# A two-layer graph network: messages laid out in steps of 32 columns, edge networks in two row halves, inputs a chunk ahead

## The chip, the cores and the metric

One core of a Trainium2 chip runs the whole program. The metric is device time in microseconds (us) of one execution. Engines are named as the profile names them: PE (TensorE) with its weight loads PEld, DVE (VectorE), ACT (ScalarE), POOL (GpSimd) and SP (SyncE, which issues most plain DMAs).

## The reference, cut to what matters

Two message-passing layers run over the same graph of N = 6250 nodes and E = 200,000 edges, sorted by destination. A node row x has 160 numbers: 64 scalars and 32 vectors of three components. Each layer mixes the rows linearly, gathers the mixed row of every edge's source, weights it by a small network of the edge's own inputs, multiplies by the edge's four attributes, sums per destination, mixes again, adds to x and normalizes. The message part of layer 0:

```python
weight = silu(edge_length_embedded @ W_fc1) @ W_fc2      # 10 -> 100 -> 192
w0, w1, w2, w3 = split(weight, [64, 128, 160])
gs, gv = x1s[edge_src], x1v[edge_src]
mid0a = w0 * gs * e_s
mid0b = w3 * (einsum('euc,ec->eu', gv, e_v) / SQRT3)
mid1a = w1[:, :, None] * gs[:, :, None] * e_v[:, None, :]
mid1b = w2[:, :, None] * gv * e_s[:, :, None]
agg = segment_sum(concatenate([...]), edge_dst) / sqrt(16)
```

Layer 1 has the network 64 -> 64 -> 224 and one more message, w5 * cross(gv, e_v). All arithmetic is fp32.

## The kernel before, in words

**Tiles and units.** The edges are cut into 1563 tiles of 128. The loop of `windows(i, ...)`, one call per layer, goes over units of four tiles, that is two pairs. Tiles are put in 284 groups of 12 down to 3 neighbouring tiles; the destinations of a group fit into a window of 32 nodes. Groups are short at the end, because destinations grow sparse in edges there and a window then holds fewer tiles: the last 220 tiles or so come in groups of three, so a unit there ends one or two groups.

**What a unit does.** The loop body issues, in this order, for unit u:
- `gather` (L665) of unit u+4: per tile one indirect DMA issued by POOL, which fetches 128 source rows of 160 numbers. The tile `g` has 8 buffers, each of a pair, so POOL can be four units ahead of the products.
- `weights` of unit u+2: per tile one matmul of hidden values by the second weight matrix into the PSUM tile `pw` (3 buffers of a pair).
- `hidden` of unit u+3: the first matrix on the inputs `e`, into the PSUM tile `pa` (1 buffer), then Silu on ACT (L624 in layer 0, L636 in layer 1). In layer 0 this is one matmul of 512 columns; in layer 1 the inputs of the first and the second pair lie in rows 0 to 63 and 64 to 127, and it is one of 256 columns.
- `places` (L699) and `products` (L681, L686) of unit u+2 on DVE. `places` makes per tile a 128 x 4 x 32 selector: one-hot of the edge's place in the window times one attribute. `products` makes the messages `mid`, not yet times an attribute: one instruction of 256 columns, and two (layer 0) or three (layer 1) of 192.
- `aggregate` of unit u on PE: selector of one attribute (32 columns, as weights) times a stretch of `mid`, summed in the PSUM tile `pg`; attribute c goes to partitions 32c to 32c+31, that is to column group c of the array. Layer 0 has six matmuls per tile (of 160, 96, 64, 64, 32 and 32 columns), layer 1 seven (160, 64, 96, 128, 96, 64, 32). When a group ends, ACT copies the sums to `r` (L728, L730).
- `turn` of the groups that ended in the unit before: PE transposes `r` into the PSUM tile `pt` (1 buffer; in layer 1 also four small matmuls), and DVE adds it to the standing sums `sm` and `sr` (L749, L751) at a place read from a register (L746).
- a step of node work. When all edges of a block of 128 nodes are in, `second_nodes` (layer 0) or `last_nodes` (layer 1) runs `summed`, `turn`, `mix` for it, one step a unit, through the PSUM tile `pn`. Its rows go to the table from which the next layer gathers.

**What sets the order.** PE keeps the order of the code (`keep_in_program_order`); the other engines get theirs from the scheduler of the framework, and each runs its queue in order. Two uses of one PSUM bank are kept apart by waits. Layer 1 can gather only when all rows of layer 0 are in the table, so the two layers do not overlap on POOL. The e inputs are DMAs of SP (L598, L607), issued in `hidden` when a chunk is first used: in layer 0 a chunk is one unit in three buffers, in layer 1 two units in two buffers. src indices and attributes come 48 tiles at a time (L578, L579).

**The prologue** makes layer 0's table (`turn_nodes`, `send_nodes`; PSUM tiles `pw`, `pa`, `pg`, `pn`, `pt`), checks the windows, and builds the weights `rm0`, `rr0` (copies L377 to L384) and `rm1`, `rr1` (16 small SP DMAs at L406, scaled at L411). L134 and L139 are the helpers through which all matmuls and transposes go, so the profile shows these two lines for PE, and tiles must be told apart by their names. The function `general` is for other graphs and does not run here.

Of the kernel before, what the change touches and what calls it, by code (L numbers as in the profile page):

```python
# [9 lines left out]
F32 = mybir.dt.float32  # L10
I32 = mybir.dt.int32
AF = mybir.ActivationFunctionType
OP = mybir.AluOpType
# [73 lines left out]
def kernel(ctx: ExitStack, tc: tile.TileContext, a, out):  # L87
# [17 lines left out]

    nc = tc.nc
# [5 lines left out]
    dram = ctx.enter_context(tc.tile_pool(name="dram", bufs=1, space=bass.MemoryType.DRAM))  # L112

# [62 lines left out]

    iota = const.tile([P, W], F32, name="iota")
# [22 lines left out]
    nc.gpsimd.dma_start(fc1[0][:10], a["W_fc1"])  # L200
# [35 lines left out]
    def turn_nodes(bs, x):  # L236
# [7 lines left out]
        z = psum.tile([P, 512], F32, name="pa", bufs=1)  # L244
# [11 lines left out]
    def send_nodes(bs, xt, zt):  # L256
# [3 lines left out]
        for j in range(len(bs)):  # L260
            tag, k = (("pg", 2), ("pn", 1), ("pg", 2), ("pt", 1))[j]
            p = psum.tile([P, 512], F32, name=tag, bufs=k)
            q = p[:n, :2 * D].rearrange("p (w d) -> p w d", w=2)
            matmul(q[:, :, 0:P], xt[:, j * P:j * P + n], l1, start=True, stop=True)
            qs.append(q)
# [50 lines left out]
    def checked():  # L316
        p = psum.tile([P, 512], F32, name="pa", bufs=1)
# [51 lines left out]
    for j in range(2):  # L369
# [3 lines left out]
        for k in range(2):  # L373
# [5 lines left out]
    nc.vector.tensor_copy(rm0[0:64, 1:4, :, S:],  # L379
                          q[0:64, None, :, S:].to_broadcast([64, 3, 2, V]))  # L380
    nc.vector.tensor_copy(rm0[64:96, 1:4, :, 0:S],
                          q[64:96, None, :, 0:S].to_broadcast([32, 3, 2, S]))
# [10 lines left out]
    for at, n, f in ((0, 160, 0.125), (160, 32, r3 / 8), (192, 32, r2 / 8)):  # L393
# [4 lines left out]
    pieces = [(rm1[0:64, 0, ss], l2s[0:64]), (rm1[64:96, 0, vx], l2v[64:96]),  # L398
              (rm1[96:128, 0, vy], l2v[64:96]), (rr1[0:32, vz], l2v[64:96])]
    pieces += [(rr1[32 * c:32 * c + 32, ss], l2s[64:96]) for c in (1, 2, 3)]  # L400
    pieces += [(rm1[0:64, 1 + c, v], l2v[0:64]) for c, v in enumerate((vx, vy, vz))]

    for c, v0, v1 in ((1, vz, vy), (2, vz, vx), (3, vy, vx)):
        pieces += [(rm1[64:96, c, v0], l2v[96:128]), (rm1[96:128, c, v1], l2v[96:128])]
# [3 lines left out]
    for o, f in ((rm1[:, :, 0:96], fs), (rm1[:, :, 96:], fv), (rr1[:, 0:96], fs),  # L408
                 (rr1[:, 96:], fv), (rm1[64:96, 1, vz], -1.0), (rm1[96:128, 2, vx], -1.0),
                 (rm1[64:96, 3, vy], -1.0)):  # L410
        nc.vector.tensor_scalar(o, o, f, None, op0=OP.mult)  # L411
# [95 lines left out]
    def last_nodes(b, work, clear):  # L507
# [10 lines left out]
        def summed():  # L518
# [5 lines left out]
            for c in (1, 2, 3):  # L524
                matmul(q[:, 96:192], sm[:, c, rows], rm1[:, c, 96:192], start=False, stop=(c == 3))
# [20 lines left out]
    def windows(i, loads, work):  # L546
        nw = (192, 224)[i]

        at_c, at_d, at_f, at_a, at_b, wid = ((0, 64, None, 160, 224, 320),
                                             (0, 160, 64, 256, 320, 416))[i]  # L550

        if i == 0:
            sums = [(0, at_a, 0, 1, 160, 0), (1, 0, 0, 1, 96, 0), (2, 0, 0, 1, 64, 0),
                    (3, 0, 0, 1, 64, 0), (2, at_d + V, 0, 1, V, 64), (3, at_d + 2 * V, 0, 1, V, 64)]
        else:
            sums = [(0, at_a, 0, 1, 160, 0), (1, 0, 0, 1, 64, 0), (2, 0, 0, 1, 96, 0),
                    (3, 0, 0, 1, 128, 0), (1, at_f + V, 0, 1, 96, 64),
                    (2, at_f + 2 * V, 2 * V, 2, V, 96), (3, at_d + 2 * V, 0, 1, V, 128)]
        made = {}
        ec = (EC // 2, EC)[i]  # L560

        inputs_of = None
        if i == 0:

            inputs_of = [loads.tile([P, EC * P // 2], F32, name=f"e{k}", bufs=1) for k in range(3)]
            for e in inputs_of:
                nc.vector.memset(e, 0.0)
# [24 lines left out]
        def inputs(c):  # L592

            e0 = c * ec * P
            n = min(ec * P, E - e0)
            if i == 0:
                e = inputs_of[c % 3]
                nc.sync.dma_start(e[:10, :n], a["e10"][:, e0:e0 + n])  # L598
            else:

                e = loads.tile([P, EC * P // 2], F32, name="e", bufs=2)
                for u in range(0, n, 4 * P):
                    for h in range(2):
                        r = u + h * 2 * P
                        m = min(2 * P, n - r)
                        if m > 0:
                            nc.sync.dma_start(e[h * 64:h * 64 + 64, u // 2:u // 2 + m],  # L607
                                              a["e64"][:, e0 + r:e0 + r + m])
            made["e", c] = e

        def hidden(u):

            t0 = 4 * u
            c = t0 // ec
            if ("e", c) not in made:
                inputs(c)
            e = made["e", c]
            n = min(4 * P, E - t0 * P)
            p = psum.tile([P, 512], F32, name="pa", bufs=1)
            h = work.tile([P, 512], F32, name="h", bufs=2)  # L620
            at = (t0 % ec) * P
            if i == 0:
                matmul(p[:100, :n], fc1[0], e[:, at:at + n], start=True, stop=True)
                nc.scalar.activation(h[:100, :n], p[:100, :n], AF.Silu)  # L624
            else:
                at //= 2
                k = P if n > 2 * P else 64
                m = min(n, 2 * P)
# [4 lines left out]
                for kk, c0, c1 in parts:  # L633
                    matmul(p[:kk, c0:c1], fc1[1][:kk, :kk], e[:kk, at + c0:at + c1],
                                     start=True, stop=True)
# [3 lines left out]
        def weights(p):  # L639

            pw = psum.tile([P, 512], F32, name="pw", bufs=3)
            q = pw.rearrange("p (j d) -> p j d", j=2)
            h = made["h", p // 2]
            for j in range(2):
# [345 lines left out]
```

## Time and profile before

| | us |
|---|---|
| median of three runs (4136.02 to 4146.30) | 4143.48 |
| the profiled execution | 4137.19 |
| its span, first to last instruction | 4135.4 |
| first and last gather of layer 0, start and end | 66.9 and 2089.8 |
| first and last gather of layer 1, start and end | 2137.3 and 4101.3 |
| granted clock of TensorE, mean | 0.911 |

The span is what the views below cover; the execution is 1.8 us longer. In a line of instruction groups the columns are line, engine, operation, out<-in, shape, count, then busy us and mean ns of one, then idle time of the engine just before them with what ended it. In a timeline the columns are start, length, engine, line, operation, tiles, shape and count, with idle time before it in brackets; consecutive instructions of one kind are merged. Instructions of one engine overlap by some 70 to 100 ns, so a mean duration is longer than the distance between two starts.

### The profile page before, as it was taken

The page shows a single profiled execution, that of the slowest core. Times are in us where ns is not written, and L with a number is a line of the kernel's source. Part 1 is how long each engine was busy: PE and PEld are TensorE (multiplying, and loading weights), DVE is VectorE, ACT ScalarE, POOL GpSimd, SP SyncE. Part 2 cuts the span into 40 slices and gives each one's busy share as a digit, 9 for nine tenths or more (in the row PEclk, how much of TensorE's full clock was granted, in tenths as well). Part 3 has the DMA queues.
Part 4 walks back from the last instruction along what each step waited for, and adds up shares of the span by engine and source line. Part 5 has one row for each costly group of instructions (what it writes and reads, how often), then busy time and mean ns, then how long its engine had stood idle before and what let it go on. Part 6 is the DMA issues. An engine that isn't in the chain of part 4 may idle for free.

```text
span 4135.4 us, 137335 instructions
## 1 busy us (share of the span) xinstructions
PE 3570.4 (86%) x53817; PEld 2582.1 (62%) x53817; DVE 2959.6 (72%) x10845; ACT 947.6 (23%) x2386; POOL 3013.5 (73%) x3232
## 2 busy tenths in 40 slices
PE   7878888889999999999988888888888788888877
PEld 5555566566666666666666666666666566666655
DVE  6766666667677777677657777777777777778887
ACT  2111111222223333333320011111112122222233
POOL 4777777777777777776637777777777777777775
PEclk8999999999999999999988888888898899888898
DMA  4222222332333333322223333333333333333432
GB/s 131 72 73 77 75 78 76 80 80 79 82 82 83 85 81 85 83 79 78 76 60 96 92 101 100 98 97 102 101 97 106 101 105 105 105 105 99 111 107 71
DMA packets 301525, 371.47 MB, mean 90 GB/s; under 512 B 86987, under 2 KB 245212, under 8 KB 300872
## 3 DMA queue, kind: packets, MB, share of 16 engines
q0 software_dynamic: 151056, 257.36, 23.6%
q1 hardware_dynamic: 121192, 88.36, 7.5%
q10 hardware_dynamic: 28624, 16.88, 1.3%
q8 instruction: 430, 7.05, 0.7%
q14 instruction: 223, 1.83, 0.1%
HBM read 341.49 MB, written 20.80 MB: 88 GB/s over the span
## 4 chain that ended last, share of the span: by engine, by line
PE 38%; issue 18%; DMA 17%; POOL 13%; DVE 12%; DVEq 1%; SPq 0%; ACT 0%; POOLq 0%; ACTq 0%
DMA g<-table,src 15%; POOL g L665 13%; PE pw L134 12%; PE pg L134 10%; PE pa L134 7%; PE pn L134 6%; DVE mid L686 4%; DVE sel L699 2%; PE pt L139 2%; DVE mid L681 2%; DMA e<-in_e 1%; PE pn L139 1%; DVE sm L749 1%; DVEq L746 1%; DVE nx L442 1%
## 5 line engine op out<-in xcount | busy, mean ns | idle before, releaser
L665 POOL DMA_INDIRECT g<-table,src x3126 | 2991.9, 957 | 1082.9 <-issue 752.5
L134 PE MATMUL pw<-fc,h 100*128 100x192 f32 (+1 forms) x6252 | 1272.9, 377 | 220.8 <-DVE mid L686 191.3
L134 PEld LDWEIGHTS pg<-mid,sel 128*32 128x32 f32 x40638 | 943.1, 118 | 490.4 <-issue 478.2
L134 PEld LDWEIGHTS pw<-fc,h 100*128 100x128 f32 (+1 forms) x6252 | 941.5, 201 | 380.3 <-issue 206.6
L686 DVE TENSOR_TENSOR mid<-g,pw 128x192 f32<-128x192 f32 x3910 | 1168.6, 346 | 0.0
L681 DVE TENSOR_TENSOR mid<-pw,g 128x256 f32<-128x256 f32 x1564 | 659.5, 422 | 697.4 <-DMA g<-table,src 441.7
L134 PE MATMUL pg<-mid,sel 128*32 128x64 f32 (+4 forms) x40638 | 1144.7, 255 | 0.0
L699 DVE SCALAR_TENSOR_TENSOR sel<-iota,off,ea 128x128 f32<-128x128 f32 x3126 | 956.6, 344 | 189.5 <-PE pg L134 156.9
L134 PE MATMUL pa<-e,fc 128*100 128x512 f32 (+1 forms) x1566 | 737.5, 555 | 117.3 <-DMA e<-in_e 117.0
L624 ACT ACTIVATE h<-pa 100x512 f32<-100x512 f32 x391 | 233.4, 597 | 1059.2 <-PE pa L134 1043.0
L134 PEld LDWEIGHTS pa<-e,fc 128*100 128x100 f32 (+1 forms) x1566 | 263.3, 192 | 247.9 <-issue 131.3
L636 ACT ACTIVATE h<-pa 128x256 f32<-128x256 f32 x392 | 150.0, 383 | 1138.9 <-PE pa L134 1127.3
L139 PE MATMUL pt<-ident,r 128*96 128x128 f32 (+1 forms) x852 | 230.3, 293 | 15.5 <-DVE sr L751 15.5
L749 DVE TENSOR_TENSOR sm<-pt,sm 96x128 f32 (+1 forms) x568 | 162.2, 286 | 106.6 <-PE pt L139 96.1
L728 ACT ACTIVATE r<-pg 128x96 f32<-128x96 f32 (+1 forms) x568 | 155.7, 274 | 360.1 <-PE pg L134 246.9
L139 PEld LDWEIGHTS pt<-ident,r 128*96 128x96 f32 (+1 forms) x852 | 106.4, 125 | 130.5 <-issue 58.7
L134 PE MATMUL pn<-rm,sm 96*128 96x128 f32 (+4 forms) x980 | 155.6, 312 | 17.0 <-DVE sm L749 15.8
L134 PEld LDWEIGHTS pn<-rm,sm 96*128 96x128 f32 (+3 forms) x980 | 148.8, 212 | 24.6 <-DVE sm L749 19.8
L134 PE MATMUL pt<-ident,r 128*32 128x32 f32 x2272 | 86.1, 205 | 56.7 <-DVE sr L751 47.4
L134 PEld LDWEIGHTS pt<-ident,r 128*32 128x32 f32 x2272 | 90.5, 120 | 61.8 <-issue 60.1
L440 ACT ACT_TABLE_LOAD x96 | 123.2, 1283 | 6.3 <-DVE mv L439 4.6
L134 PE MATMUL pn<-rr,sr 64*128 64x128 f32 (+2 forms) x196 | 58.5, 383 | 70.5 <-DVE sr L751 70.5
(132 smaller groups left out, 1227.5 us busy)
## 6 DMA issues: line engine op xcount, KB each, us to landing
g<-table,src POOLq DMA_INDIRECT x3126
e<-in_e SPq DMA_DIRECT2D x781, 64.0 KB
e<-in_e SPq DMA_DIRECT2D x390, 20.0 KB
ea<-in_ea_main SPq DMA_DIRECT2D x63, 96.0 KB
xself<-no ACTq DMA_DIRECT2D x48, 96.0 KB
no<-xself SPq DMA_DIRECT2D x48, 96.0 KB
xg<-in_x_main SPq DMA_DIRECT2D x12, 320.0 KB
table<-rg SPq DMA_DIRECT2D x12, 320.0 KB
```

Source lines behind the costliest of these rows:

```text
L134: r = nc.tensor.matmul(*args, **kw)
L139: r = nc.tensor.transpose(*args)
L440: nc.scalar.activation(mv[:n, 1:2], mv[:n, 1:2], AF.Sqrt, bias=eps[:n])
L442: nc.vector.tensor_scalar(y, y, mv[:n, 0:1], mv[:n, 1:2], op0=OP.subtract, op1=OP.mult)
L624: nc.scalar.activation(h[:100, :n], p[:100, :n], AF.Silu)
L636: nc.scalar.activation(h[:kk, c0:c1], p[:kk, c0:c1], AF.Silu, scale=0.125)
L665: nc.gpsimd.indirect_dma_start(out=g[:n, j, :], out_offset=None, in_=table[i][:, :], in_offset=bass.IndirectOffsetOnAxis(ap=of(t)[0], axis=0))
L681: nc.vector.tensor_tensor(two, q[:n, :m, 0:2 * S].rearrange("p j (k d) -> p j k d", k=2), gs, OP.mult)
L686: nc.vector.tensor_tensor(o[:, :, at:at + 96].rearrange("p j (c d) -> p j c d", c=3), gv, q[:n, :m, None, w0:w0 + V].to_broadcast([n, m, 3 ...
L699: made["last"] = nc.vector.scalar_tensor_tensor(s[:n, j], iota[:n, None, :].to_broadcast([n, 4, W]), w, e[:, :, None].to_broadcast([n, 4, ...
L728: nc.scalar.activation(r[:, :w], pg[:, :w], AF.Copy)
L749: nc.vector.tensor_tensor(sm[:h, :, at], pt[:h, :P].rearrange("p (c w) -> p c w", c=4), sm[:h, :, at], OP.add)
```

## The change

Four things are changed, and the results are the same.

1. **Messages in steps of 32 columns.** `mid` is laid out in blocks of 32 columns, so placed that what one attribute needs is at equal steps: one matmul per attribute and tile, four instead of six or seven. The blocks of one product are no longer neighbours, so DVE makes them in more instructions: per pair 128, 128, 192, 192 columns in layer 0, and 128, 128, 192, 128, 64, 192 in layer 1. The weights `rm0`, `rm1`, `rr1` are permuted to fit.
2. **Edge networks in two halves of the rows.** Layer 0's inputs are laid into rows 0 to 9 and 64 to 73, and `hidden` becomes two matmuls of 256 columns, one on each half of the array's rows, into two banks of a new PSUM tile `pair`, with one Silu each. In layer 1 `weights` takes the two pairs in turn, so consecutive matmuls use different halves.
3. **Inputs a chunk ahead.** Both layers have chunks of two units in three shared buffers, and `hidden` asks for chunk c+1 when it first uses c.
4. **PSUM.** `pair` (two banks) takes the place of `pa` and `pt`: `hidden` uses columns 0 to 255, and `turn` columns 256 to 511 of bank g % 2. In layer 1 the four small matmuls of `turn` become one: ACT copies the last 32 columns of each attribute to the diagonal blocks of a 128 x 128 tile `rest`, and one matmul by `fold` adds them up.

```diff
+    pair = psum.tile([P, 2, 512], F32, name="pair", bufs=1)
...
+    fold = const.tile([P, W], F32, name="fold")
+    nc.vector.tensor_reduce(fold, ident.rearrange("p (c w) -> p w c", w=W), AX.X, OP.add)
+    rest = [const.tile([P, P], F32, name=f"rest{k}") for k in range(3)]
+    for t in rest:
+        nc.vector.memset(t, 0.0)
...
-    nc.gpsimd.dma_start(fc1[0][:10], a["W_fc1"])
+    for r in (0, 64):
+        nc.gpsimd.dma_start(fc1[0][r:r + 10], a["W_fc1"])
...
-        z = psum.tile([P, 512], F32, name="pa", bufs=1)
+        z = pair[:, 0, 0:P]
...
-    nc.vector.tensor_copy(rm0[0:64, 1:4, :, S:],
-                          q[0:64, None, :, S:].to_broadcast([64, 3, 2, V]))
-    nc.vector.tensor_copy(rm0[64:96, 1:4, :, 0:S],
-                          q[64:96, None, :, 0:S].to_broadcast([32, 3, 2, S]))
+    for c, at_c, at_d in ((1, (32, 64), 0), (2, (0, 64), 32), (3, (0, 32), 64)):
+        for k, r in enumerate(at_c):
+            nc.vector.tensor_copy(rm0[r:r + 32, c, :, S:], q[32 * k:32 * k + 32, :, S:])
+        nc.vector.tensor_copy(rm0[at_d:at_d + 32, c, :, 0:S], q[64:96, :, 0:S])
...
+    for c, parts in enumerate(rows):
+        pieces += [(rm1[32 * k:32 * k + 32, c, v], w) for k, (w, v) in enumerate(parts[:4])]
+        pieces.append((rr1[32 * c:32 * c + 32, parts[4][1]], parts[4][0]))
...
-                matmul(q[:, 96:192], sm[:, c, rows], rm1[:, c, 96:192], start=False, stop=(c == 3))
+                v = slice(96 if c == 2 else 0, 192)
+                matmul(q[:, v], sm[:, c, rows], rm1[:, c, v], start=False, stop=(c == 3))
...
+        scalar = lambda w, place: (w, V, 0, 2, place, 2)
+        vector = lambda w, place, step, c=0, n=3: (w, 0, S + c * V, n, place, step)
+        kinds = ((scalar(0, 2), scalar(S, 5), vector(128, 9, 2), vector(160, 0, 3)),
+                 (scalar(0, 2), scalar(S, 10), vector(128, 9, 2), vector(160, 5, 3, 0, 2),
+                  vector(160, 1, 1, 2, 1), vector(192, 0, 3)))[i]
+        sums = (((5, 2, 5), (0, 2, 3), (2, 1, 3), (2, 2, 3)),
+                ((9, 1, 5), (2, 1, 5), (0, 2, 5), (0, 1, 5)))[i]
...
+            e = inputs_of[c % 3]
+            for h in range(2):
+                if i == 0 and n == EC * P:
+                    nc.sync.dma_start(
+                        e[h * 64:h * 64 + k].rearrange("p (u m) -> p u m", m=2 * P),
+                        of_e[:, e0:e0 + n].rearrange("p (u h m) -> p u h m", h=2, m=2 * P)[:, :, h])
+                    continue
...
-            if ("e", c) not in made:
-                inputs(c)
+            for k in (c, c + 1):
+                if ("e", k) not in made and k * EC < NT:
+                    inputs(k)
...
-                matmul(p[:100, :n], fc1[0], e[:, at:at + n], start=True, stop=True)
-                nc.scalar.activation(h[:100, :n], p[:100, :n], AF.Silu)
+                halves = [(0, m)] + [(1, n - m)] * (n > m)
+                for j, m in halves:
+                    k = slice(64 * j, 64 * j + 64)
+                    matmul(pair[:100, j, :m], fc1[0][k], e[k, at:at + m], start=True, stop=True)
+                for j, m in halves:
+                    nc.scalar.activation(h[:100, 2 * P * j:2 * P * j + m], pair[:100, j, :m], AF.Silu)
             else:
-                at //= 2
+                p = pair[:, u % 2]
...
+            for w, w_step, c, k, place, step in kinds:
                 nc.vector.tensor_tensor(
-                    o[:, :, at:at + 96].rearrange("p j (c d) -> p j c d", c=3), gv,
-                    q[:n, :m, None, w0:w0 + V].to_broadcast([n, m, 3, V]), OP.mult)
+                    parts(mid[:n, :m], V * place, V * step, k), parts(g[:n, :m], c, V, k),
+                    parts(q[:n, :m], w, w_step, k), OP.mult)
...
-            for q, (c, c0, step, k, w, at) in enumerate(sums):
+            for c, (at, step, k) in enumerate(sums):
+                o = mid[:n, t % 2, V * at:V * at + V]
+                o = bass.AP(tensor=o.tensor, offset=o.offset, ap=[o.ap[0], [V * step, k], [1, V]])
+                matmul(pg[32 * c:32 * c + 32, :k * V], s[:n, t % 2, c, :], o,
+                       start=first, stop=last, tile_position=(0, 32 * c))
...
+                    for c in range(4):
+                        k = slice(32 * c, 32 * c + 32)
+                        nc.scalar.activation(rest[g % 3][k, k], pg[k, P:P + V], AF.Copy)
...
-            pt = psum.tile([P, 512], F32, name="pt", bufs=1)
+            pt = pair[:, g % 2, 2 * P:]
...
-                for c in range(4):
-                    k = slice(32 * c, 32 * c + 32)
-                    matmul(pt[k, P:P + W], r[:, P:P + W], ident[:, k],
-                           start=True, stop=True, tile_position=(0, 32 * c))
                 transpose(pt[:, :P], r[:, :P], ident)
+                matmul(pt[:, P:P + W], rest[g % 3], fold, start=True, stop=True)
```

## The prediction, made before the changed kernel was built or run

> **What bounds the kernel now.** I read the page first. PE is the busiest engine, but the share of POOL has to be read with the gap between its instructions.
>
> ```profile
> PE 3570.4 (86%) x53817; PEld 2582.1 (62%) x53817; DVE 2959.6 (72%) x10845; ACT 947.6 (23%) x2386; POOL 3013.5 (73%) x3232
> ...
> L665 POOL DMA_INDIRECT g<-table,src x3126 | 2991.9, 957 | 1082.9 <-issue 752.5
> ```
>
> The timeline of POOL shows that gap. Two neighbouring gathers start 1.25 us apart, 0.95 busy and 0.30 idle, even where nothing is waited for; the third one here is late by 1 us.
>
> ```profile
> 1990.22 0.95 POOL L665 DMA_INDIRECT g<-table,src  x1 [0.30 <-DVE nx L462]
> 1991.47 0.95 POOL L665 DMA_INDIRECT g<-table,src  x1 [0.30 <-issue]
> 1993.77 0.94 POOL L665 DMA_INDIRECT g<-table,src  x1 [1.34 <-DVE sel L699]
> ```
>
> So 1563 gathers take 1955 us a layer at least, 5.006 a unit, and the change does not touch them. Layer 0 takes 2022.9 (66.9 to 2089.8). Summing every distance between starts above 1.35 us gives 60.8 us of late gathers there, 47.6 of it after 1700 us; layer 1 takes 1964.0, with 6.7 late. So the span is 66.9 before the first gather, 2 x 1955 of gathers, 60.8 and 6.7 late, 12 of slightly longer gathers, 47.5 between the layers and 34.1 after the last. Only 149 us of the whole is not gathers or the prologue.
>
> Who makes the gathers late? The waits of POOL and of PE between 1700 and about 2090, and the same stretch in the table by windows (PE, PEld, DVE, ACT, POOL busy):
>
> ```profile
> POOL g L665 <- DVE mid L686: 57.5, 51, 3.2
> ...
> PE pt L139 <- DVE sr L751: 13.5, 22, 0.8
> ```
>
> ```profile
> 1700.00:2090.00 390.00, 364.75 (x4549) 253.39 (x4548) 272.02 (x1005) 131.57 (x382) 263.70 (x273) 0.97 0.29 78
> 3400.00:4101.00 701.00, 576.60 (x10810) 437.94 (x10810) 560.75 (x2193) 193.18 (x438) 531.61 (x557) 0.89 0.39 105
> ```
>
> POOL waits for products to free `g`, but DVE is busy only 70% there and PE 94%: late layer 0 is bound by PE. The 47.6 us over 68 units mean a PE cycle of 5.006 + 0.70 = 5.7 us. From 3400 on POOL is the bound, with DVE at 80%. The timeline of PE gives the pieces of a late unit with two turns:
>
> ```profile
> 1967.61 1.57 PE L134 MATMUL pw<-fc,h 100*128 100x192 f32 x8
> 1969.02 1.02 PE L134 MATMUL pa<-e,fc 128*100 128x512 f32 x2
> 1969.97 1.27 PE L134 MATMUL pg<-mid,sel 128*32 128x160 f32 x48
> 1971.17 0.46 PE L139 MATMUL pt<-ident,r 128*96 128x128 f32 x2
> 1972.20 0.43 PE L139 MATMUL pt<-ident,r 128*96 128x128 f32 x2 [0.56 <-DVE sr L751]
> ```
>
> By distances of starts: weights 1.40, hidden 0.95, aggregate 1.205, a turn 0.39, a second turn 1.0 with its wait. A plain unit is 3.95; a unit with `mix` 5.59, with the self part 5.06, with `summed` 6.50.
>
> **The change part by part.**
>
> *Fewer matmuls in `aggregate`.* Layer 0 drops 16 of 48 records a unit (each fp32 matmul is two records), layer 1 24 of 56. The Trainium skill, page "TensorEngine Tiling (Array Packing)", section "Instruction Overhead", puts about 60 cycles on every matmul; at the 2.4 GHz of the page "TensorE: Matmul & The Clock Gate" that is 25 ns, so by the rule 0.40 us a unit, 27 us over the 68 late units. The records say otherwise: in a unit of layer 0 the eight 160-column records of column group 0 start 136 ns apart, and 8 x 0.136 = 1.09 of the block's 1.205; the rest (0.117) is entering and leaving. The other groups' records run beside them (96 columns 83 ns, 64 columns 56, 32 columns 31). The widest group sets the block and stays 160 wide: I take 0. In layer 1 the widest group is 128 + 32 columns in two records, 142 ns against 136: 0.05 us of 1.26.
>
> *Hidden in two row halves.* Two 256-column matmuls at 0.433/2 = 0.217 per record (0.433 is the distance in the 512-column pair), running side by side: 0.43, plus 0.09 for leaving as now, 0.52 against 0.954. That would save 0.43 us a unit. The same page, "Key Properties", speaks against it: changing the tiling mode drains TensorE. Rows near it are those of layer 1, which already goes from half rows to full rows:
>
> ```profile
> 3866.81 1.03 PE L134 MATMUL pw<-fc,h 64*128 64x224 f32 x8
> 3867.77 0.70 PE L134 MATMUL pa<-e,fc 128*128 128x256 f32 x2
> 3868.40 1.31 PE L134 MATMUL pg<-mid,sel 128*32 128x160 f32 x55
> ...
> 3875.42 0.27 PE L134 MATMUL pt<-ident,r 128*32 128x32 f32 x8 [2.19 <-DVE sr L751]
> ```
>
> `pa` there takes 0.63 for 0.43 of streaming: 0.107 to enter, 0.09 to leave, and `pw` pays 0.09 to leave. So layer 0 would have `pw` 1.40 + 0.09 and hidden 0.64: 2.13 against 2.36, a saving of 0.22. Bounds 0.1 and 0.43; I take 0.22, by the row. The first lines also show the eight half-row records of layer 1 done in 0.96, about 4 x 188 ns + 0.2: they overlap already in the old order, so the new order of `weights` is worth 0 late; earlier PE only waits there.
>
> *`pt` in two banks.* A second turn no longer waits for DVE's addition: 0.56 each, 22 times, 12 us in late layer 0. In layer 1 that wait is longer (2.19 above). Four small matmuls for one of 128 rows: 0.447 a turn now, about 0.26 + 2 x 0.11 after: 0. The four ACT copies a group (0.2 each by L730's 32-partition row) lie a unit before their turn.
>
> *New waits.* `pt` shares a bank with hidden: it must wait for Silu to have read the bank, and hidden for DVE's addition of the turn before. Behind the first on PE are node steps and the next `weights`. Silu comes about 0.07 after hidden and takes 0.6 to 0.8; aggregate covers 1.2. Not where ACT loads a table first (1.28 us, once a block, in the unit where PE waits about 0.55 for the normalized row anyway): between 0 and 1 us there, and I give that unit no saving from hidden instead. The second wait is covered by `weights` (1.4); uncovered it would be 0.4.
>
> *Products.* Starts of DVE's instructions back to back are 341 ns apart for 256 columns, 264 for 192, 201 for a 128-column addition from PSUM (L749), 98 for 32. Per pair layer 0 goes from 0.87 to 2 x 0.20 + 2 x 0.264 = 0.93, layer 1 from 1.13 to 3 x 0.20 + 2 x 0.264 + 0.13 = 1.26: 0.13 and 0.27 us a unit. POOL's 5.006 hides it (DVE 3.8 to 4.2 busy a unit). Uncovered it costs 0.27 a unit where DVE is the bound.
>
> *Inputs ahead.* PE waits for e inputs 117 us in all, none of it in the late stretch of layer 0; POOL's lead of four units hides the rest: 0. As many SP issues as before. SP's wait for a free buffer stands three units ahead of use, as now, and what queues behind it (src, attributes, node rows) keeps its distance.
>
> *Prologue.* Four more SP DMAs at L406 at 0.55 (2.2; the chain of waits passes through L406), seven more DVE copies at 0.2 against 0.9 for two now (+1.1), fold and memsets at the start beside DMA waits, one more POOL DMA within its 40 us of idling. 0 to 3.5; I take 2.5. Two widened matmuls in `last_nodes`: 0.3 us a block, hidden but for the last: 0.
>
> *The sum.* The products' lag behind the gather now grows from 4 us at 1591 to 19 at 1815; POOL stalls only from about 19 on, when `g` is used up. Carrying each late unit's PE time forward with these savings (0.22 in three units of four, 0.56 per second turn; mean late cycle 5.7 to about 5.35), the lag is 5 to 9 at 1815 and fills near the end: 8 us late, and with the stretches at lowered clock (a unit then grows by about 2 us, some six times) about 18. So 60.8 becomes 18: -43. The lag at the end is nearly the same, so the 47.5 between the layers loses 1. Layer 1 and tail: DVE's 0.27 against the vanished turn waits, +2. Prologue +2.5. In all -39.5: 4137.2 becomes 4097.7, and the median, 6.3 above the profiled execution, 4104.
>
> **The rivals.**
>
> *Layer 1 becomes bound by DVE (slower).* In the last 100 units the lag already grows from 2.5 to 12, a loop of 5.1 us; 0.27 more in full is 0.37 above POOL (36 us), and the 80 units before at 4.95 + 0.27 give 17. Less the 19 - 3 of room, about 37 late and 7 more at the end: +44. If DVE also holds the turns in layer 0, only 15 is won there: 4143.5 + 44 - 15 + 2.5 = 4175. It decides when DVE's units with their waits pass 5.006. Against it: PE's waits for `sr`, up to 2.2 us in every third late unit, go away, and products are then the only work between. Chance 0.12.
>
> *The halves bring nothing (same).* Drains at 0.43 a unit or `pt` behind Silu eat hidden's saving; only the second turns gain: -15 + 2.5, 4131, about no change. Chance 0.20.
>
> *The halves cost no drain (faster).* PE then falls to 5.1 a unit, the lag never fills, 58 of the 60.8 go, and 8 of the 47.5: 4080. Chance 0.18.
>
> The main case has 0.50.
>
> **The numbers.** A measurement of this kernel can tell about 0.3%, 12 us: faster is below 4131. The main case (4090 to 4118 by itself) and the third give 0.68, half of the second adds a little: 0.70. Same 0.18, slower 0.12. The range goes from the third case to just past the second, 4076 to 4146.
>
> **What would show it.** Right: gathers of layer 0 late by under 25 us in all, `pw` to `pg` 2.13 us in a plain unit, aggregate still 1.2 in both layers, no idle PE before a second `pt`, layer 1's last gather still about 1964 after its first. Wrong: late gathers in layer 1 behind `mid`, PE idle at `pt` behind ACT in every unit, or an aggregate block well under 1.2.

## The result, and the profile after

The changed kernel takes 4151.4 us, the median of 16 runs (4139.5 to 4162.3), against 4137.4 for the kernel before on the same chip. The ratio over all runs is 1.0021, with a 95% interval of 1.0011 to 1.003 (the two medians alone would give 1.0034): a loss about as small as the 0.3% that was called no change. The forecast was 4104, in a range of 4076 to 4146; its sign and its range are both wrong.

The page of the changed kernel, as that of before (busy us, share, instructions; in a line of groups busy us, mean ns, idle us before):

```profile
PE 3476.9 (84%) x37265; PEld 2397.6 (58%) x37265; DVE 3103.4 (75%) x13202; ACT 1151.1 (28%) x3915; POOL 3018.9 (73%) x3233
...
L681 POOL DMA_INDIRECT g<-table,src x3126 | 2997.0, 959 | 1088.9 <-issue 722.5
```

A third of PE's instructions is gone, and PE's busy time has fallen by only 94 us; DVE's has grown by 144. POOL still issues 3126 gathers, so the division of the span used in the prediction still holds. Here it is for the changed kernel and for two experiments told below. For the changed kernel it is a second profile, from the last set of runs and another chip: its gathers start 1.251 us apart, as before. In the first profile they started 1.254 us apart, which alone is 9.4 us over 3126 gathers; as both are the same kernel, that is not the change's.

| us | before | changed | one turn bank | two tiles |
|---|---|---|---|---|
| to the first gather | 66.9 | 77.3 | 68.2 | 67.7 |
| gathers of layer 0 | 2022.9 | 1999.9 | 1994.2 | 1986.6 |
| between the layers | 47.5 | 51.4 | 51.4 | 49.4 |
| gathers of layer 1 | 1964.0 | 1972.4 | 1972.0 | 1965.6 |
| after the last gather | 34.1 | 39.5 | 39.7 | 30.2 |
| span | 4135.4 | 4140.4 | 4125.4 | 4099.5 |

Layer 0 gains 23, and everything else loses 28: 10 in the prologue, 4 between the layers, 8 in layer 1, 5 at the end. The table by windows of the changed kernel (PE, PEld, DVE, ACT, POOL busy, then the granted clock) and its waits from 1700 to 2090 (us in all, times, longest) answer to those of before:

```profile
1700.00:2090.00 390.00, 359.82 (x3697) 254.23 (x3694) 285.92 (x1170) 139.34 (x462) 274.12 (x281) 0.97 0.30 81
3400.00:4101.00 701.00, 558.48 (x6375) 390.63 (x6375) 582.67 (x2682) 283.75 (x1048) 526.92 (x549) 0.91 0.38 103
```

```profile
POOL g L681 <- DVE mid L699: 38.2, 40, 4.1
...
PE pair L143 <- DVE sr L761: 12.5, 22, 0.9
PE pair L143 <- ACT h L643: 10.8, 13, 0.9
```

PE is as full as before in late layer 0, and still waits for `sr` 22 times in front of a transpose, 12.5 us in all, as in the kernel before (13.5). A wait for Silu (`h`) has come on top. The timeline of PE in such a unit, as that of before (start, length, instruction, idle time before it):

```profile
1914.97 1.57 PE L138 MATMUL pw<-fc,h 100*128 100x192 f32 x8
1916.46 0.68 PE L138 MATMUL pair<-e,fc 64*100 64x256 f32 x4
1917.07 1.27 PE L138 MATMUL pg<-mid,sel 128*32 128x160 f32 x32
1918.28 0.46 PE L143 MATMUL pair<-ident,r 128*96 128x128 f32 x2
1919.27 0.46 PE L143 MATMUL pair<-ident,r 128*96 128x128 f32 x2 [0.53 <-DVE sr L761]
```

By distances of starts weights and hidden take 2.10 us (forecast 2.13), and the aggregate, now of 32 records, 1.21 (forecast unchanged at 1.205). Those two steps hold. The last line does not: the second turn writes the other bank of `pair` and waits 0.53 us all the same. Layer 1 has the same wait, longer, and the prologue has one that was not there before: the transpose of `xz` goes to bank 0 of `pair` and waits for DVE to read bank 1 (before, first line; changed, second and third):

```profile
50.73 0.27 PE L139 MATMUL pa<-ident,xz 128*128 128x128 f32 x1
```

```profile
52.65 0.33 PE L143 MATMUL pair<-ident,xz 128*128 128x128 f32 x1 [1.18 <-DVE rg L286]
...
3909.72 0.33 PE L143 MATMUL pair<-ident,r 128*128 128x128 f32 x1 [1.53 <-DVE sr L761]
```

So theory A: `pair` is one tile, waits are kept for the whole tile, and an access to one bank waits for another engine's last access to the other bank. Rival B: these waits are the data's own, or cover something that ends later anyway. Rival C: DVE's additional instructions hold both layers.

### The profile page after: what moved, and what is told of

Read it like the earlier page. It is cut to its first block, busy times and chain, and to the rows that moved or that the text cites. A ratio compares the mean times of both kernels' runs of the same rounds, so it can differ in the third digit from the quotient of the medians.

```text
span 4151.9 us, 108120 instructions
## 1 busy us (share of the span) xinstructions
PE 3476.9 (84%) x37265; PEld 2397.6 (58%) x37265; DVE 3103.4 (75%) x13202; ACT 1151.1 (28%) x3915; POOL 3018.9 (73%) x3233
## 4 chain that ended last, share of the span: by engine, by line
PE 29%; issue 21%; DMA 16%; POOL 15%; DVE 15%; ACT 2%; DVEq 1%; SPq 0%; ACTq 0%; POOLq 0%
DMA g<-table,src 16%; POOL g L681 15%; DVE mid L699 9%; PE pw L138 8%; PE pn L138 7%; PE pg L138 7%; PE pair L138 4%; DVE sel L712 2%; PE pair L143 2%; DVE sm L759 1%; DVEq L756 1%; PE pn L143 1%; ACT L458 1%; DVE sr L761 0%; DVE nx L460 0%
## 5 line engine op out<-in xcount | busy, mean ns | idle before, releaser
L699 DVE TENSOR_TENSOR mid<-g,pw 128x128 f32<-128x128 f32 (+2 forms) x7820 | 1857.1, 302 | 679.5 <-DMA g<-table,src 463.2
L138 PE MATMUL pw<-fc,h 100*128 100x192 f32 (+1 forms) x6252 | 1188.2, 383 | 133.9 <-DVE mid L699 126.0
L138 PE MATMUL pg<-mid,sel 128*32 128x160 f32 (+1 forms) x25008 | 1170.5, 311 | 0.0
L138 PEld LDWEIGHTS pw<-fc,h 100*128 100x128 f32 (+1 forms) x6252 | 870.2, 203 | 301.3 <-issue 233.6
L138 PEld LDWEIGHTS pg<-mid,sel 128*32 128x32 f32 x25008 | 782.4, 119 | 400.6 <-issue 320.0
L138 PE MATMUL pair<-e,fc 64*100 64x256 f32 (+1 forms) x2348 | 612.2, 467 | 301.3 <-DVE sr L761 288.1
L138 PEld LDWEIGHTS pair<-e,fc 64*100 64x100 f32 (+1 forms) x2348 | 242.4, 188 | 533.7 <-DVE sr L761 369.9
L643 ACT ACTIVATE h<-pair 100x256 f32<-100x256 f32 x782 | 257.6, 381 | 1018.9 <-PE pair L138 980.3
L654 ACT ACTIVATE h<-pair 128x256 f32<-128x256 f32 x392 | 150.5, 384 | 1021.4 <-PE pair L138 1018.7
L143 PE MATMUL pair<-ident,r 128*96 128x128 f32 (+1 forms) x852 | 227.5, 290 | 104.7 <-DVE sr L761 49.7
L143 PEld LDWEIGHTS pair<-ident,r 128*96 128x96 f32 (+1 forms) x852 | 105.5, 124 | 288.5 <-issue 99.1
L759 DVE TENSOR_TENSOR sm<-pair,sm 96x128 f32 (+1 forms) x568 | 163.2, 287 | 90.8 <-PE pair L143 33.2
L743 ACT ACTIVATE rest<-pg 32x32 f32<-32x32 f32 x1136 | 209.6, 184 | 12.5
L138 PE MATMUL pn<-rm,sm 96*128 96x128 f32 (+4 forms) x980 | 179.5, 339 | 26.7 <-DVE sm L759 25.4
L138 PEld LDWEIGHTS pn<-rm,sm 96*128 96x128 f32 (+3 forms) x980 | 164.9, 222 | 35.6 <-DVE sm L759 29.1
L138 PE MATMUL pn<-rr,sr 64*128 64x128 f32 (+2 forms) x196 | 62.0, 403 | 53.5 <-DVE sr L761 51.6
L138 PEld LDWEIGHTS pair<-fold,rest 128*128 128x128 f32 x568 | 106.4, 229 | 0.0
```

What stands on the lines that cost most here:

```text
L138: r = nc.tensor.matmul(*args, **kw)
L143: r = nc.tensor.transpose(*args)
L643: nc.scalar.activation(h[:100, 2 * P * j:2 * P * j + m], pair[:100, j, :m], AF.Silu)
L654: nc.scalar.activation(h[:kk, c0:c1], p[:kk, c0:c1], AF.Silu, scale=0.125)
L699: nc.vector.tensor_tensor(parts(mid[:n, :m], V * place, V * step, k), parts(g[:n, :m], c, V, k), parts(q[:n, :m], w, w_step, k), OP.mult)
L743: nc.scalar.activation(rest[g % 3][k, k], pg[k, P:P + V], AF.Copy)
```

## The experiments

The experiments ran in sets, each on one chip with the kernel before beside it. The two-tile kernel ran in the first set and in the last; kernels of other sets are compared with it by their ratios to the kernel before. PE's order is that of the code, but the scheduler makes the order of DVE and ACT anew for each kernel: between the changed kernel and the two tiles, PE's order is the same, DVE's differs in 366 of 13202 places, and ACT's in 75 of 3915, none of these between 1700 and 2090 us (two tiles against one turn bank, below: the same, 342 and 28). What such differences are worth here was not tried.

**Two tiles.** `pair` becomes two tiles of one bank each; every instruction keeps its bank and its data, and PE its order.

```diff
-    pair = psum.tile([P, 2, 512], F32, name="pair", bufs=1)
+    pair = [psum.tile([P, 512], F32, name=f"pair{k}", bufs=1) for k in range(2)]
...
-                    matmul(pair[:100, j, :m], fc1[0][k], e[k, at:at + m], start=True, stop=True)
+                    matmul(pair[j][:100, :m], fc1[0][k], e[k, at:at + m], start=True, stop=True)
...
-            pt = pair[:, g % 2, 2 * P:]
+            pt = pair[g % 2][:, 2 * P:]
```

> The changed kernel with one edit: `pair`, one tile of two PSUM banks, becomes two tiles of one bank each; every instruction keeps its place, its bank and its data. Theory A (the waits were bookkept for the whole tile, so an access to one bank waited for the other engine's last access to the other bank): first gather at about 68.5 us instead of 78.9, second `pt` of a unit without idle time, late gathers of layer 0 about 20 us instead of 40.6, time 4115 to 4125. Theory B (the waits are the data's own, or hidden behind the other engines): 4145 to 4155, as the changed kernel. Theory C (DVE's additional product instructions hold both layers): only the prologue comes back, 4139 to 4143, and layer 1's gathers still span 1975 or more.

4095.6 against 4132.2: ratio 0.9907 (0.9893 to 0.9922). The first gather comes at 65.8, late gathers of layer 0 add up to 21.8 us, layer 1's gathers span 1965.6. That is 20 us below A's range (layer 1 and the tail, which it left as they were, gained too), and far from B and C. So the one-tile form is what costs, though A had its price too low. In a second profile of it the two turns of a unit are now one piece of four records without idle time:

```profile
1801.35 1.27 PE L138 MATMUL pg<-mid,sel 128*32 128x160 f32 x32
1802.55 0.85 PE L143 MATMUL pair<-ident,r 128*96 128x128 f32 x4
1803.33 1.57 PE L138 MATMUL pw<-fc,h 100*128 100x192 f32 x8
```

**Messages only.** The kernel before with item 1 of the change alone: the diff's `kinds`, `sums`, `products`, `rm0` and `rm1` (and two input tiles shared by the layers).

> The kernel before with only the new message layout (four matmuls a tile, messages in steps of 32 columns, the two additional DVE instructions a pair in all, the prologue's new copies and loads); layer 1's inputs use two of the three input tiles of layer 0, to fit the memory. Theory A: DVE's 0.13 and 0.27 us a unit are hidden by POOL's 5.006, so only the prologue's 2 to 3.5 us: 1 to 5 us above the kernel before, layer 1's gathers span 1964 to 1967. Theory C: layer 1's gathers span 1974 or more, 12 to 20 us above the kernel before.

4139.1 against 4132.2, ratio 1.0031 (1.0014 to 1.0047). First gather 68.7, layer 1's gathers 1966.1. The time alone doesn't decide: six of the ten runs took 4136 to 4141 and four 4152 to 4161, so the median is 6.8 us above, a little over A's 1 to 5, but the ratio stands for 6 to 19. The span of layer 1 does: it is in A's range, and C asked for 1974 or more. It comes from one of the shorter runs; what makes the four longer is not known. The two-tile kernel, which has the same instructions of DVE, shows 1965.6 in both of its profiles, so they are hidden there.

**Two tiles, old messages.** The opposite: the two-tile kernel with item 1 undone.

> The two-tile kernel with the old message layout put back (48 and 56 matmul records a unit in the aggregate, three or four product instructions a pair as before); it keeps the row halves, the inputs ahead, the two banks and the new turn of layer 1. Theory A: 0 to 4 us below the two-tile kernel (only the prologue's loads and copies differ). Theory C: the whole gain of the other edits shows, 4090 to 4105, and at least 20 us below the two-tile kernel.

4138.7, ratio 1.0013 (1.0005 to 1.0021): 43 us above the two-tile kernel, where A expected 0 to 4 below and C a gain. Neither. The timeline of ACT, then that of PE, in one of its late units:

```profile
1894.71 0.38 ACT L640 ACTIVATE h<-pair 100x256 f32<-100x256 f32 x1 [4.30 <-PE pair L138]
1895.12 1.28 ACT L454 ACT_TABLE_LOAD   x1
1896.41 0.29 ACT L454 ACTIVATE mv<-mv,eps 128x1 f32<-128x1 f32 x1
1896.72 1.28 ACT L640 ACT_TABLE_LOAD   x1
...
1898.02 0.39 ACT L640 ACTIVATE h<-pair 100x256 f32<-100x256 f32 x1
```

```profile
1898.46 0.89 PE L143 MATMUL pair<-ident,r 128*96 128x128 f32 x4 [2.57 <-ACT h L640]
```

The scheduler put the square root of the normalization (L454) between the two halves of Silu, in all 13 blocks between 1700 and 2040. The second half then waits for two table loads, and `pt`, which shares its bank, with it. In the two-tile kernel the square root stands in front of both halves. The kernels differ in the layout and in this place at once, so the order was set by hand in the next run.

**Old messages, square root first.**

```diff
-        nc.scalar.activation(mv[:n, 1:2], mv[:n, 1:2], AF.Sqrt, bias=eps[:n])
+        root["last"] = nc.scalar.activation(mv[:n, 1:2], mv[:n, 1:2], AF.Sqrt, bias=eps[:n])
...
+                    with tc.issue_after(root["last"].ins) if root else ExitStack():
```

> The two-tile kernel with the old message layout once more, with ACT's queue put in the order that the two-tile kernel has: the square root of a block's normalization in front of the first Silu of the next unit, instead of between its two halves, where all 13 late ones of layer 0 stood (then the second half, and the turn that shares its bank, wait for two table loads, up to 2.57 us of idle PE). If the place of the square root made the 43 us between the two kernels: layer 0's late gathers 20 to 30 us instead of 67, 4095 to 4108. If the additional matmul records themselves cost the time (a lower granted clock or their own length): late gathers still over 45 us, 4120 to 4140.

4092.1 against 4131.2, ratio 0.99 (0.9882 to 0.9918), late gathers of layer 0 17.2 us. By the ratios, the place of one ACT instruction was worth some 46 us, and the new message layout brings no gain: the two-tile kernel, which has it, is at 0.9907.

**Square root behind Silu.** The two-tile kernel with root, reciprocal and scaling moved into the next step, behind both halves.

```diff
+        def turn():
+            scaled(st["x"][:n], st["mv"])
```

> The two-tile kernel with the square root, the reciprocal and the scaling of a block of layer 0 moved one step later, behind both Silu of the next unit, so that no Silu stands behind a table load while PE is about to want its bank. The idle 0.60 to 0.73 us before `pt` once a block (9 us in the late stretch of layer 0) should go, and the wait of the normalized row's transpose grow to 0.1 to 0.4 us: late gathers of layer 0 13 to 22 us, 4088 to 4097. If the root then comes later than PE wants the row: 4098 to 4106.

4138.2, ratio 1.0019 (1.0012 to 1.0026): a miss, far above both cases. No `pt` waits for Silu now, but the transpose of the normalized row does wait for the root, 1.69 us a block. From 1700 to 2040 (us in all, times, longest):

```profile
PE pn L143 <- DVE nx L468: 21.9, 13, 1.9
```

**Full rows.** The two-tile kernel with hidden of layer 0 on all rows, one half after the other.

```diff
-                    matmul(pair[j][:100, :m], fc1[0][k], e[k, at:at + m], start=True, stop=True)
+                    matmul(pair[j][:100, :m], fc1[2 * j], e[:, at:at + m], start=True, stop=True)
```

> The two-tile kernel with layer 0's hidden on all 128 rows: still two matmuls of 256 columns into the two banks with one Silu each, but each with its own weights that are zero outside its ten rows, so the two do not run side by side. By the prediction's row a unit costs 0.22 to 0.25 us more on PE (hidden 0.95 against 0.61, weights 1.40 against 1.50), 15 to 17 us over 68 late units, of which the room of 19 us of lag hides some: 4101 to 4112, late gathers of layer 0 27 to 38 us. If the halves bring nothing and the banks alone do: 4093 to 4099.

4116.4, ratio 0.9963 (0.9948 to 0.9979), 4 us over the expected range; late gathers 37.6. By distances of starts weights and hidden take 1.40 and 0.96 here, against 1.50 and 0.61 in the changed kernel above, so the halves save 0.25 us a unit:

```profile
1802.51 1.57 PE L138 MATMUL pw<-fc,h 100*128 100x192 f32 x8
1803.91 1.03 PE L138 MATMUL pair<-e,fc 128*100 128x256 f32 x4
1804.87 0.73 PE L138 MATMUL pg<-mid,sel 128*32 128x160 f32 x16
```

That is what the prediction's row promised, and it is worth some 20 us.

**Not ahead, and the old rest.** The two-tile kernel with inputs asked for at first use (`for k in (c,)`), and with layer 1's turn by four small matmuls.

> The two-tile kernel with a chunk of inputs asked for when it is first used, not a chunk ahead (chunks and buffers as they are). By the prediction the lead of POOL hides these waits: within 3 us of the two-tile kernel, with PE waiting for e for some 100 us in all. If the inputs ahead carry part of the gain: 4105 or more, and late gathers in the first half of a layer.

> The two-tile kernel with layer 1's turn as before (four small 32-column matmuls by a column group each, one 160-column ACT copy, no `rest` and `fold`). If the four ACT copies a group and the 128-row matmul are hidden, as the prediction has it: within 3 us of the two-tile kernel, layer 1 the same. If the copies hold Silu and with it PE: layer 1's gathers span at least 5 us less.

In this order 4097.0 (0.9913, 0.9895 to 0.993) and 4098.1 (0.9914, 0.9901 to 0.9926): both parts are worth nothing that can be measured, as forecast. The first expectation also named a wait of some 100 us for `e`; PE waits only 5.8 us for it there (117 in the kernel before), so without asking ahead it is gone too, probably by the larger chunks of layer 0.

**The whole tile in the kernel before.** `pa` and `pt`, two tiles, become the two banks of one, and nothing else changes in the code.

```diff
+    pair = psum.tile([P, 2, 512], F32, name="pair", bufs=1)
...
-            pt = psum.tile([P, 512], F32, name="pt", bufs=1)
+            pt = pair[:, 1]
```

> The kernel before with one edit: `pa` and `pt`, two tiles of one bank each, become the two banks of one tile; nothing else changes, and each access stays in its own bank. Theory A (waits are kept for the whole tile): the prologue's `xz` transposes wait for the copies out of the other bank, so the first gather comes at 75 to 79 us instead of 67; in layer 0 `pt` waits for Silu and hidden for `sr`, so its late gathers grow from 61 to 65 to 80 us (a second `pt` waited for `sr` before already); 4143 to 4165 in all, against about 4131 for the kernel before. Theory B (the waits are the data's own): as the kernel before, within 4 us, first gather at 67.

> The same kernel as in the run before this one (the kernel before, with `pa` and `pt` as the two banks of one tile), since that chip granted TensorE a clock of 0.75 to 0.77 to both kernels and took 6515 us for the kernel before. On a chip with a clock near 0.9, theory A expects as before: first gather at 75 to 79 us, late gathers of layer 0 65 to 80 us, ratio 1.003 to 1.008. Theory B: ratio 1.000 within 0.001, first gather at 67.

The second run gave 4146.6 against 4131.2, ratio 1.0033 (1.0016 to 1.0049), first gather at 78.0, with the new wait in the prologue:

```profile
52.17 0.33 PE L140 MATMUL pair<-ident,xz 128*128 128x128 f32 x1 [1.17 <-DVE rg L274]
```

A holds without any other part of the change: the prologue alone is 11.1 us longer. But late layer 0 didn't move (60.3 us of late gathers against 60.8): there A's expectation was wrong. The second turn of this kernel waits for `sr` by its data already, and the waits that are new cost nothing there. The first run gave 1.0332 (1.0301 to 1.0363), 6722.7 against 6515.0, with a granted clock of 0.75 to 0.77 in both (told at the end).

**One turn bank.** The two-tile kernel with `pt = pair[1]` always: the second turn waits by its data, and the waits across two banks stay away. It also puts every turn into the bank of the second half of Silu. Its first two runs met the low clock too; the third is in one set with the changed kernel, the two tiles, and the old messages with the root first.

> The two-tile kernel with every turn in the same bank, so that a second turn of a unit has to wait for DVE's addition of the first by its data, as it does in the changed kernel by the bookkeeping; the prologue stays as in the two-tile kernel. If the second turns carry the difference in the layers, as the prediction's step has it (0.56 us each, 22 times in late layer 0): late gathers of layer 0 30 to 42 us instead of 22, layer 1's gathers span 1966 to 1974, 4104 to 4120. If only the waits of hidden and of the prologue count: as the two-tile kernel within 4 us.

> The same kernel as in the run before this one (the two-tile kernel with every turn in one bank), since that chip too granted TensorE a clock of only 0.76. On a chip with a clock near 0.9: if the second turns carry the difference in the layers, late gathers of layer 0 30 to 42 us, layer 1's gathers span 1966 to 1974, ratio 0.993 to 0.997; if only the waits of hidden and of the prologue count, ratio 0.990 to 0.992, as the two-tile kernel.

> The changed kernel, as it is, as the base of this set. With a clock near 0.9: ratio 1.001 to 1.003 to the kernel before. With a clock near 0.76, where PE is the bound throughout: the halves save their 0.22 to 0.25 us a unit everywhere, 100 us a layer 0, and the whole-tile waits take about half of it back: ratio 0.95 to 0.97.

> The changed kernel with `pair` as two tiles, again. With a clock near 0.9: ratio 0.990. With a clock near 0.76: below the kernel with one turn bank (0.914 and 0.920 in its two runs) if second turns count there, 0.89 to 0.91; equal to it if they don't.

> The two-tile kernel with every turn in one bank, again. If second turns carry the difference in the layers: nearer to the changed kernel than to the two-tile kernel. If the waits of hidden and `pt` carry it: within a quarter of the distance of the two-tile kernel.

> The two-tile kernel with the old message layout and the square root in front of both Silu, again. With a clock near 0.9: ratio 0.990, as the two-tile kernel. With a clock near 0.76: the same as the two-tile kernel within 0.5% if the widest column group sets the block, as the prediction has it; 2% or more above it if every matmul record costs time of its own (16 and 24 records a unit at 25 ns each, by the rule that the prediction cites, would be 0.4 and 0.6 us a unit, some 390 us in all).

| one chip, kernel before 4132.0 | median us | ratio (95%) |
|---|---|---|
| changed | 4140.4 | 1.0019 (1.0011 to 1.0028) |
| one turn bank | 4132.1 | 1.0003 (0.9992 to 1.0013) |
| two tiles | 4098.6 | 0.9919 (0.9906 to 0.9933) |
| old messages, root first | 4085.0 | 0.9895 (0.988 to 0.991) |

The low-clock runs gave 6088.5 against 6672.2 (0.9141) and 5996.4 against 6512.3 (0.9199); with no other kernel of the set beside them they tell nothing on the second turn. In the set of the table 42 us lie between the changed kernel and the two tiles. By the medians 34 of them come with the single turn bank and 8 with the prologue and the other whole-tile waits; by the profiled executions (the table of spans above) 26 and 15. That is more than expected: the ratio is 1.0003, where 0.993 to 0.997 was forecast. PE's waits over the whole span are below, of the changed kernel, of one turn bank and of two tiles (L138 is hidden, L143 a turn, `h` L643 the Silu of layer 0):

```profile
PE pair L138 <- DVE sr L761: 299.5, 220, 3.0
PE pair L143 <- DVE sr L761: 51.3, 51, 2.8
PE pair L143 <- ACT h L643: 37.2, 34, 3.1
...
PE pair L138 <- DVE sr L761: 162.9, 138, 2.7
PE pair L143 <- DVE sr L761: 60.0, 52, 3.0
PE pair L143 <- ACT h L643: 37.0, 32, 2.6
...
PE pair L138 <- DVE sr L761: 143.8, 120, 2.4
PE pair L143 <- ACT h L643: 22.6, 25, 2.6
```

With two tiles no turn waits for `sr`. But one turn bank also waits longer for Silu than two tiles do, so its 26 to 34 us are not the second turn alone. Hidden's waits for `sr` in the changed kernel, the longest of all, must be covered nearly whole: of the 8 to 15 us, some 9 are the prologue. The one-turn-bank kernel shows the idle time of the changed kernel again, now by the data:

```profile
1798.08 0.46 PE L143 MATMUL pair<-ident,r 128*96 128x128 f32 x2
1799.08 0.46 PE L143 MATMUL pair<-ident,r 128*96 128x128 f32 x2 [0.54 <-DVE sr L761]
```

The version with the old messages and the root first beats the kernel before in both of its sets, and the changed kernel in this one. Here it is 13.6 us below two tiles; in the earlier sets, where the two ran on different chips, 3.5. Whether the new layout costs a few us is not settled.

## Why the prediction was wrong, by its own steps

**The step that failed** is "*`pt` in two banks.* A second turn no longer waits for DVE's addition". It counted banks; what waits are kept for is the tile, and the diff shows `pair` as one tile. With that one step put right the gain is there: -35.9 us in the span, where the sum said -39.5. Nearly all that went wrong in size comes from there:

- *Prologue*, forecast +2.5: +10.4. The costed copies and loads are small (two tiles: +0.8 and -1.1 in two profiles). What I had left out is that `z` and the fourth of the group's products became banks of one tile: 1.17 us in nearly every chunk of the prologue, in a loop that sets the first gather.
- *Layer 0*, forecast -43: -23.0. With two tiles it is -36.3 and -37.6 in two profiles. Of the 13.3 between changed and two tiles, 7.6 come with the single turn bank and 5.7 with the other waits of the tile (the table, one turn bank between them).
- *Between the layers*, forecast -1: +3.9; with two tiles +1.9 and -1.0.
- *Layer 1 and the tail*, forecast +2: +8.4 and +5.4. With two tiles +1.6 and -3.9. The sum let DVE's 0.27 us a unit be paid by "the vanished turn waits"; they had not vanished. The single turn bank makes nearly all of it: 6.4 us in layer 1 and 9.5 after the last gather, between one turn bank and two tiles in the table. Why the same wait costs nothing in layer 1 of the messages-only kernel (1966.1), I can't say; hidden there does not wait for `sr`, and its turn is the old one.

**What held.** With two tiles the span is 35.9 and, in the first profile, 41.9 us below that of before; by the medians of the two sets 33 and 37. That the total comes so near is in part luck: in the second profile layer 0 gains 7 less than forecast and the stretch between the layers loses 3, while the prologue is 2 better and layer 1 with the tail 4. In the division of the span, the slightly longer gathers come to 9 us, not 12; nothing rests on it. *Fewer matmuls* at 0: the block is 1.205 us with 48 and with 32 records. By the rule that the prediction cites, of about 60 cycles a matmul, the old messages would have been some 27 us slower in late layer 0; their late gathers are 17.2 and 14.4 us in two profiles, against 21.8 and 24.2 with two tiles. *Hidden in two row halves* at 0.22 us a unit: 0.25. *Products* hidden by POOL, *inputs ahead* at 0, the new *rest* at 0. The rival in which layer 1 becomes bound by DVE (4175) fell with the two tiles: layer 1's gathers span 1965.6 with all of DVE's new instructions. The rival in which the halves bring nothing came nearest in time (4131), but not by its reason: `pt` behind Silu is there, 10.8 us from 1700 to 2090, yet it did not take the gain, and the halves brought theirs. The rival with no drain (4080) falls: entering and leaving the halves is paid (1.50 for 1.40, 0.61 for 0.43), as the row of layer 1 said.

**A price that the sum lacked.** An idle PE loses more than the idle time. Four stretches of 3.41 us around the 2.57 us of idle time shown above for the two-tile kernel with old messages, by the table by windows (length, PE, PEld, DVE, ACT, POOL busy, clock):

```profile
1892.24:1895.65 3.41, 3.41 (x62) 2.62 (x62) 2.95 (x11) 0.92 (x2) 1.70 (x3) 1.00 0.17 48
1895.65:1899.06 3.41, 0.84 (x5) 0.35 (x3) 1.43 (x7) 2.76 (x5) 2.50 (x4) 1.00 0.25 72
1899.06:1902.48 3.42, 3.42 (x14) 2.83 (x13) 1.68 (x7) 0.72 (x4) 0.69 (x1) 0.50 0.20 53
1902.48:1905.89 3.41, 3.41 (x49) 1.83 (x51) 1.57 (x5) 1.40 (x6) 2.78 (x3) 0.50 0.35 91
```

The stretch with the idle time still runs at the full clock, the next two at half. So 2.57 us of waiting costs up to 3.4 us more, an estimate from the two stretches at half clock. The same table from 1700 to 2040, for this kernel and for the same one with the root moved:

```profile
1700.00:2040.00 340.00, 307.36 (x3950) 219.42 (x3952) 229.39 (x853) 116.59 (x379) 224.30 (x233) 0.92 0.28 76
1700.00:2040.00 340.00, 320.73 (x4384) 231.67 (x4383) 253.15 (x943) 130.45 (x428) 255.36 (x263) 0.99 0.32 87
```

The clock differs by 7%, which over 340 us is 24 us of lost clock, and PE is idle 13 us longer (32.6 against 19.3). If both go straight into the time, they answer to most of the 46; that the clock's share does was not tried by itself.

## What to carry to other kernels

Before counting on two banks as independent, look at how the program names them: two slices of one tile are one thing to the waits, and two tiles are two. When an edit that should be free costs 40 us, compare the order of the queues first; one square root with its table loads, moved between two halves, cost 46 us, about as much as two tiles gain over one (42). A gain counted in one step that rests on a wait having gone elsewhere should be listed once, with all that falls if that wait stays.

## What the runs showed of the hardware that was not expected

The granted clock is 1.0 or 0.5 in every record of every profile, and within a profile all its changes but the last lie on one grid of 3.413 us. Late layer 0 (1700 to 2040) of five profiles (before, changed, two tiles, old messages with the root between and in front) can be cut into those steps, and the steps at full clock sorted by how long PE was idle in them:

| idle PE in a step at full clock | next step at half clock |
|---|---|
| under 0.5 us | 0 of 363 |
| 0.5 to 1.0 us | 9 of 75 |
| 1.0 to 1.5 us | 6 of 19 |
| over 1.5 us | 8 of 8 |

The ends of matmuls are modelled in the profile, so single cases may move by a class. The Trainium skill ("TensorE: Matmul & The Clock Gate", section "What's actually happening") gives the same window, 3413 ns, and the same half clock, but has the clock halve after at least one idle window; here idle time of less than half a window, added up, was enough, and the measurement decides.

In three runs TensorE was granted a mean of only 0.75 to 0.77, for the kernel before as well, which then took 6512 to 6672 us. Gathers were late there from the start (1327 us in layer 0 of the one-tile version), the one-tile version lost 3.3% instead of 0.3%, and the one-turn-bank version gained 8 to 9% instead of nothing. The low clock may be a result and not the cause: PE is busy for only 72 to 75% of the span in the three profiles, and in the one-tile version it stands 510 us in front of `aggregate`'s records with nothing that the profile shows to wait for. It is not one chip's property either: the third of these runs was on a chip that had granted 0.91 to 0.92 to the same kernel before in an earlier set. What does that was not tried.
